# Splitting the last batch's residual, feed-forward and output into two token halves, in an LSH-attention plus FFN kernel

## The chip, the cores and the metric

The kernel runs on one core of a Trainium2 chip. The metric is the device time of one execution in microseconds (us). A core has five engines that each work through their own instruction queue in order: TensorE (PE, matrix products), VectorE (DVE), ScalarE (ACT, activation functions), GpSimd (POOL) and SyncE (SP, which here issues the DMAs). They wait for one another by semaphores.

## The reference, cut to what matters

There are 16 batches of 512 tokens with 128 features. Each batch goes through an attention block and a feed-forward block, both with a layer norm before and after and a residual around:

```python
x = x + ln(attn(ln(x)))          # 16 heads of 8; softmax over scores times a bucket coefficient
x = x + ln(ffn(ln(x)))
# attn: q, v from two 128x128 products; buckets are the signs of q against 6 hyperplanes
#       scores = q q^T / sqrt(128); coeff = 62 + (bucket_s == bucket_t); softmax(scores*coeff) v
# ffn:  h = silu(x W1^T * s1) * (x W2^T * s2)      128 -> 512
#       h = gelu(h H1^T * t1);  h = gelu(h H2^T * t2)   512 -> 512, twice
#       y = h W3^T * s3                            512 -> 128
```

All of it is float32 outside; the scores use a split of q in three bfloat16 parts.

## The kernel before

**Tiling.** A batch is held as `[128, NT, E]` with `NT = 4`: partition p holds tokens 4p to 4p+3, so "tile t" means every fourth token. A norm works tile by tile over 128 features. In the FFN the tokens lie along the free axis: `xnt` is `[128, 512]`, `h` is `[128, NC, 512]` with `NC = 4` blocks ("c") of hidden units. One hidden block of a 512x512 layer is four products (i = 0 to 3) accumulated in one PSUM bank, and a float32 product is two MATMUL instructions in the trace.

**Order of the work.** The program is written by a small planner, the class `Order`. Every piece of the kernel is a Python generator that yields operations (`pe`, `dve`, `act`, `pool`, `dma`), each with an assumed cost, a rank and a function that emits the instructions. The planner advances an assumed clock and lets each engine take the ready operation of lowest rank, first come first served within a rank. ACT takes the one with the lowest time ready plus rank, with 4 us added if it needs another function table. What comes out is one fixed order for each engine; on the chip the engines follow it and wait only for their data. Ranks on PE are 0 for scores, 1 for the weighing with v, 2 for projections and transposes, 4 for the FFN: the FFN fills what attention leaves.

**Buffers are taken in the plan.** `get(pool)` waits in the plan until a named buffer is put back, in order of asking. The pools that matter here: `banks` (2 PSUM banks for transposes, normed values, weighing), `ffn_banks` (3 PSUM banks), `h_bufs` (3), `a_bufs` (2, for the SiLU results), `x1_bufs` (2, the sum after attention, held until the batch's output is added), `xnt_bufs` (1, the transposed input of the FFN).

**From attention to output, for each batch b.** `attend` weighs four heads at a time and ends in `divide` (L1004, L1005), which fills a quarter of the tile `o`. After the fourth, `residual(b)` reloads x (tile `xtr`, L1026), and then:

1. `moments(o)`: statistics of o (DVE, L430 and L434), variance plus eps (ACT, L446, `ve_o`), power -1/2 (POOL, L450, `rs_o`), negated mean times that (DVE, L455, `nm_o`).
2. `rescale` of o into a PSUM bank (ACT, L473, `yb`), and only then `get(x1_bufs)`; the add into `x1` (DVE, L1035).
3. `get(xnt_bufs)`, then `norm_transposed`: moments of x1 (`ve_f`, `rs_f`, `nm_f`), `xn_f` (ACT), four PE transposes (L489, `tp_f`), one copy to `xnt_f` (ACT, L493).
4. `ffn(b)` waits until the previous batch has its first 512x512 layer planned (`stages[b - 1][AHEAD]`). Then come the first-stage products with W1 and W2 (PE, L1088, tile `w`), SiLU in pairs (ACT, L1074), the product of the two (DVE, L1057), two layers of 16 products (PE, L1122, `hp`) with GELU in pairs (ACT, L1135), and the last product (PE, L1156, `yp`, 32 MATMULs of 128x128).
5. The output norm: sums and squares of yp (ACT, L397 and L407), `ve_y`, `rs_y`, `nm_y`, `yn` (L473), the add of x1 (DVE, L1180), after which x1's buffer is put back, and one output DMA (L1186).

The pieces of the attention that fill the engines meanwhile are the logits (DVE, L894), the coefficients (DVE, L865), the subtraction of the maximum (POOL, L947), the exponential (ACT, L952), the scores (PE, L847) and the weighing (PE, L973).

```python
    x1_bufs = Pool("x1_", 2)          # residual(b): taken after rescale, before the add at L1035
    xnt_bufs = Pool("xntf", 1)        # residual(b): taken after that add
    ...
    ffn_banks = Pool("f", 3)          # gate, hp, yp: one bank each
```

Of the kernel before, what the change touches and what calls it, by code (L numbers as in the profile page):

```python
# [190 lines left out]
def tile_lsh_attention_ffn(  # L191
# [193 lines left out]
    def moments(src, name, rank, copy=None):  # L385


        q = name[0]
        rs = p2.tile([P, NT], F32, tag=f"rs{q}", name=f"rs_{name}")
        nm = p2.tile([P, NT], F32, tag=f"nm{q}", name=f"nm_{name}")  # L390
        if copy is not None:

            sums = p2.tile([P, 2, NT], F32, tag=f"su{q}", name=f"su_{name}")

            def sum_(ts_):
                for t in ts_:
                    nc.scalar.activation(  # L397
                        copy[0][:, t, :],
                        src[:, t, :],
                        AF.Identity,  # L400
                        scale=ROOT / E,
                        accum_out=sums[:, 0, t : t + 1],
                    )

            def square(ts_):
                for t in ts_:
                    nc.scalar.activation(  # L407
                        junk,
                        src[:, t, :],
                        AF.Square,  # L410
                        scale=-1.0 * E,
                        bias=sums[:, 0, t : t + 1],
                        accum_out=sums[:, 1, t : t + 1],
                    )

            yield act(1.0, -2, lambda: sum_((0, 1)))
            yield act(1.0, -2, lambda: sum_((2, 3)))
            src = copy[0]
            copy[1]()
            yield act(1.2, -2, lambda: square((0, 1)))  # L420
            od.loose()
            yield act(1.2, -2, lambda: square((2, 3)))
            mean, var = sums[:, 0, :], sums[:, 1, :]
            factor, sign = float(E) ** -3, -1.0 / E
        else:
            st = p2.tile([P, NT, nc.vector.BN_STATS_DIM], F32, tag=f"st{q}", name=f"st_{name}")

            def stats(ts_):
                for t in ts_:
                    nc.vector.bn_stats(st[:, t, :], src[:, t, :])  # L430

            def aggr():
                for t in range(NT):
                    nc.vector.bn_aggr(mv[:, t, :], st[:, t, :])  # L434

            yield dve(0.46, rank, lambda: stats((0, 1)))
            od.loose()
            yield dve(0.46, rank, lambda: stats((2, 3)))
            mv = p2.tile([P, NT, nc.vector.BN_AGGR_DIM], F32, tag=f"mv{q}", name=f"mv_{name}")
            yield dve(0.7, rank, aggr)  # L440
            mean, var, sign, factor = mv[:, :, 0], mv[:, :, 1], -1.0, 1.0
        ve = p2.tile([P, NT], F32, tag=f"ve{q}", name=f"ve_{name}")
        yield act(
            0.22,
            -5,
            lambda: nc.scalar.activation(  # L446
                ve, var, AF.Identity, bias=eps if factor == 1.0 else eps3, scale=factor
            ),
        )
        yield pool(1.0, 0, lambda: nc.gpsimd.tensor_tensor(rs, ve, mhalf[:, 0], op=ALU.pow))  # L450

        def negate():

            for t in range(NT):
                nc.vector.tensor_scalar(  # L455
                    nm[:, t : t + 1],
                    mean[:, t : t + 1],
                    sign,
                    rs[:, t : t + 1],
                    op0=ALU.mult,  # L460
                    op1=ALU.mult,
                )

        yield dve(0.28, rank, negate)
        return nm, rs

    def rescale(src, dst, scales):
# [13 lines left out]
        yield act(0.88, -2, lambda: emit((0, 1)))  # L481
        yield act(0.88, -2, lambda: emit((2, 3)))

    def turned(xn, xnt_tag, name, k, tp):


        def turn():
            for t in range(NT):
                nc.tensor.transpose(tp[:, ts(t, P)], xn[:, t, :], ident)  # L489

        yield pe(0.5, 2, turn)
        xnt = p1.tile([P, S], F32, tag=xnt_tag, name=f"xnt_{name}")
        yield act(0.5, -2, lambda: nc.scalar.copy(xnt, tp))  # L493
        od.put(banks, k)
        return xnt

    def norm_transposed(src, xnt_tag, name, rank):

        xn = p2.tile([P, NT, E], F32, tag=f"xn{name[0]}", name=f"xn_{name}", bufs=1)
        scales = yield from moments(src, name, rank)  # L500
        yield from rescale(src, lambda t: xn[:, t, :], scales)
        k = yield get(banks)
        return (yield from turned(xn, xnt_tag, name, k, bank(k, f"tp_{name}")))
# [78 lines left out]
    def prep(b):  # L582
# [14 lines left out]
        if b:  # L597
            yield wait(known[b])
            xn = p2.tile([P, NT, E], F32, tag="xna", name=f"xn_a{b}", bufs=1)
            yield from rescale(xt, lambda t: xn[:, t, :], (nm_x[:, b], rs_x[:, b]))  # L600
            k = yield get(banks)
            xnt = yield from turned(xn, "xnta", f"a{b}", k, bank(k, f"tp_a{b}"))
        else:
            xnt = yield from norm_transposed(xt, "xnta", f"a{b}", 1)
# [413 lines left out]
    def residual(b):  # L1018
# [10 lines left out]
        scales = yield from moments(o, f"o{b}", 1)  # L1029
        kb = yield get(banks)  # L1030
        ybt = bank(kb, f"yb_{b}").rearrange("p (t e) -> p t e", t=NT)
        yield from rescale(o, lambda t: ybt[:, t, :], scales)
        k1 = yield get(x1_bufs)
        x1 = p1.tile([P, NT, E], F32, tag=k1, name=f"x1_{b}")
        yield dve(0.6, 1, lambda: nc.vector.tensor_tensor(x1, ybt, xt, op=ALU.add))  # L1035
        od.put(banks, kb)
        kx = yield get(xnt_bufs)
        xnt = yield from norm_transposed(x1, kx, f"f{b}", 1)
        od.spawn(ffn(b, x1, k1, xnt, kx))

    def ffn(b, x1, k1, xnt, kx):
# [4 lines left out]
        kh = yield get(h_bufs)  # L1046
        h = p1.tile([P, NC, S], F32, tag=kh, name=f"h_{b}_0")
        there = events(NC)

        def product(w2, c, half, held, h=h, there=there):  # L1050
            yield wait(half)
            kb, g2 = w2
            a, ka = held[c % 2]
            yield dve(
                0.66,
                1,
                lambda: nc.vector.tensor_tensor(h[:, c, :], g2, a, op=ALU.mult),  # L1057
            )
            od.put(ffn_banks, kb)
# [3 lines left out]
        def silus(c0, gates, half, held):  # L1063
            for _ in gates:
                held.append((yield get(a_bufs)))
            tiles = [
                p1.tile([P, S], F32, tag=ka, name=f"a_{b}_{c0 + i}")
# [3 lines left out]
            def emit():  # L1071
                for i, (a, (_, gp)) in enumerate(zip(tiles, gates)):
# [3 lines left out]
            yield act(1.2, 0, emit, "silu")  # L1076
            for kb, _ in gates:
                od.put(ffn_banks, kb)
            held[:] = zip(tiles, list(held))
            od.set(half)  # L1080

        def gate(which, c):
            kb = yield get(ffn_banks)
            gp = bank(kb, f"{which}_{b}_{c}")
            yield pe(
                0.86,
                4,
                lambda: nc.tensor.matmul(  # L1088
                    gp, lhsT=w_sb[which][:, 0, ts(c, P)], rhs=xnt, start=True, stop=True
                ),  # L1090
            )
            return kb, gp

        for c0 in range(0, NC, 2):
            gates = []
            for c in (c0, c0 + 1):
                gates.append((yield from gate("w1", c)))
            half, held = Event(), []
            od.spawn(silus(c0, gates, half, held))
            for c in (c0, c0 + 1):  # L1100
                w2 = yield from gate("w2", c)
                od.spawn(product(w2, c, half, held))
        od.put(xnt_bufs, kx)
        od.set(stages[b][0])

        for layer in (1, 2):
            w = w_sb[f"h{layer}"]
            hin, khin, before = h, kh, there
            kh = yield get(h_bufs)
            h = p1.tile([P, NC, S], F32, tag=kh, name=f"h_{b}_{layer}")  # L1110
            there = events(NC)
            for c0 in range(0, NC, 2):
                got = []
                for c in (c0, c0 + 1):
                    kb = yield get(ffn_banks)
                    hp = bank(kb, f"hp_{b}_{layer}_{c}")
                    for i in range(NC):
                        yield wait(before[i])
                        yield pe(
                            0.86,  # L1120
# [4 lines left out]
                                rhs=hin[:, i, :],  # L1125
# [4 lines left out]
                    got.append((c, kb, hp))  # L1130

                def gelus(got=got, h=h, there=there, sc=w_sb[f"h{layer}s"]):
                    def emit():
                        for c, _, hp in got:
                            nc.scalar.activation(  # L1135
                                h[:, c, :], hp, AF.Gelu, scale=sc[:, c : c + 1]
                            )

                    yield act(1.2, 0, emit, "gelu")
                    for c, kb, _ in got:  # L1140
                        od.put(ffn_banks, kb)
                        od.set(there[c])

                od.spawn(gelus())
            od.put(h_bufs, khin)
            od.set(stages[b][layer])
# [4 lines left out]
        yp = bank(kb, f"yp_{b}")  # L1151
        for t in range(NT):
# [12 lines left out]
        od.put(h_bufs, kh)  # L1165
        od.set(stages[b][3])


        y = p2.tile([P, NT, E], F32, tag="y", name=f"y_{b}", bufs=1)
# [3 lines left out]
            1,  # L1173
            (y, lambda: od.put(ffn_banks, kb)),
        )
        kn = yield get(banks)
        ybt = bank(kn, f"yn_{b}").rearrange("p (t e) -> p t e", t=NT)
        yield from rescale(y, lambda t: ybt[:, t, :], scales)
        z = y
        yield dve(0.6, 1, lambda: nc.vector.tensor_tensor(z, ybt, x1, op=ALU.add))  # L1180
        od.put(banks, kn)
        od.put(x1_bufs, k1)
# [3 lines left out]
            lambda: nc.sync.dma_start(out=out[b].rearrange("(p t) e -> p t e", t=NT), in_=z),  # L1186
# [134 lines left out]
```

## Time and profile before

| what | value |
|---|---|
| three runs | 1370.01, 1375.74, 1375.81 us; median 1375.74 us |
| the profiled execution | 1373.08 us in all; its span, first to last instruction, 1371.3 us |
| granted TensorE clock | 0.991 of full speed over the span |
| busy share of the span | PE 96%, DVE 90%, POOL 89%, ACT 82% |

The profile is of one execution, so sums made from it stand against 1373.08 us (1371.3 us of span and 1.8 us around it), which is 2.7 us under the median of the runs. Times in a timeline are us from the start of the span. A line of a timeline has start, duration, engine, source line, operation, output and inputs, and how many such instructions are merged; in brackets is how long the engine sat idle before it and for whom. `PEld` is the loading of the stationary operand, which the trace lists apart from the MATMUL.

### The profile page before, as it was taken

The page shows a single profiled execution, that of the slowest core. Times are in us where ns is not written, and L with a number is a line of the kernel's source. Part 1 is how long each engine was busy: PE and PEld are TensorE (multiplying, and loading weights), DVE is VectorE, ACT ScalarE, POOL GpSimd, SP SyncE. Part 2 cuts the span into 40 slices and gives each one's busy share as a digit, 9 for nine tenths or more (in the row PEclk, how much of TensorE's full clock was granted, in tenths as well). Part 3 has the DMA queues.
Part 4 walks back from the last instruction along what each step waited for, and adds up shares of the span by engine and source line. Part 5 has one row for each costly group of instructions (what it writes and reads, how often), then busy time and mean ns, then how long its engine had stood idle before and what let it go on. Part 6 is the DMA issues. An engine that isn't in the chain of part 4 may idle for free.

```text
span 1371.3 us, 21177 instructions
## 1 busy us (share of the span) xinstructions
PE 1317.3 (96%) x5922; PEld 550.9 (40%) x5922; DVE 1236.0 (90%) x3989; ACT 1127.8 (82%) x1607; POOL 1217.1 (89%) x319
## 2 busy tenths in 40 slices
PE   9999999999889999999999999999999999999996
PEld 3433334334334434343434434343434434343443
DVE  5999999999889999999999999999999999998210
ACT  2567798999779888988989888988989888988852
POOL 1599999999999999999999999999999999999400
PEclk9999999999899999999999999999999999999998
DMA  5756455445435455445545455454545454453000
GB/s 143 194 148 157 133 150 145 140 140 141 134 106 153 125 130 142 138 138 132 147 116 147 129 134 135 139 139 135 142 124 141 135 134 135 132 122 101 24 8 8
DMA packets 159837, 175.39 MB, mean 128 GB/s; under 512 B 34280, under 2 KB 117480, under 8 KB 159720
## 3 DMA queue, kind: packets, MB, share of 16 engines
q1 hardware_dynamic: 156909, 170.56, 45.4%
q10 hardware_dynamic: 2811, 3.48, 0.8%
q8 instruction: 47, 0.77, 0.2%
q14 instruction: 70, 0.57, 0.1%
HBM read 154.81 MB, written 19.17 MB: 127 GB/s over the span
## 4 chain that ended last, share of the span: by engine, by line
PE 50%; DVE 24%; POOL 9%; issue 8%; DMA 6%; ACT 2%; SPq 1%; POOLq 0%; DVEq 0%; ACTq 0%
PE hp L1122 18%; PE av L973 12%; DVE l L894 11%; PE sp L847 9%; DVE co L865 8%; POOL l L947 8%; PE w L1088 4%; PE yp L1156 3%; DMA mb<-md 3%; DMA bb<-bkd 1%; DMA qd<-q 1%; PE op L994 1%; PE vp L760 1%; POOL rs_x L561 1%; DMA qr<-qd 1%
## 5 line engine op out<-in xcount | busy, mean ns | idle before, releaser
L947 POOL TENSOR_TENSOR l<-l,mb 128x2048 f32<-128x2048 f32 x256 | 1156.1, 4552 | 43.4 <-DVE mxpad L894 24.0
L894 DVE CUSTOM_DVE_ANT_0 l<-co,sp 128x512 f32<-128x512 bf16 x1024 | 665.7, 681 | 13.8 <-PE av L973 6.9
L952 ACT ACTIVATE l<-l 128x2048 f32<-128x2048 f32 x256 | 484.6, 1907 | 40.9 <-POOL l L947 39.4
L1122 PE MATMUL hp<-h,h 128*128 128x512 f32 x1024 | 498.6, 596 | 0.3 <-ACT h L1135 0.3
L865 DVE TENSOR_SCALAR co<-bb,bj 128x516 bf16<-128x516 bf16 x1024 | 455.0, 472 | 3.3 <-DMA bb<-bkd 3.1
L847 PE MATMUL sp<-qr,ql 72*128 72x512 bf16 x1024 | 358.0, 382 | 26.7 <-DVE mxpad L894 22.5
L1122 PEld LDWEIGHTS hp<-h,h 128*128 128x128 f32 x1024 | 190.1, 190 | 185.6 <-issue 151.6
L973 PE MATMUL av<-l,vaug 128*32 128x512 f32 x2048 | 263.6, 603 | 0.0
L847 PEld LDWEIGHTS <-ql 72*128 72x128 bf16 x1024 | 94.1, 97 | 313.9 <-issue 290.7
L1088 PE MATMUL w<-xnt_f,w 128*128 128x512 f32 x256 | 132.0, 601 | 2.5 <-ACT a L1074 2.4
L952 ACT ACT_TABLE_LOAD x86 | 110.3, 1283 | 1.5
L1251 PE MATMUL activity<-still 128*128 128x512 bf16 x402 | 106.6, 385 | 1.0 <-DVE still L280 1.0
L973 PEld LDWEIGHTS av<-l,vaug 128*32 128x32 f32 x2048 | 47.4, 109 | 116.5 <-issue 93.9
L894 DVE DVE_READ_ACCUMULATOR2_ANT mxpad<- 128x1 f32 x1024 | 85.7, 84 | 0.0
L450 POOL TENSOR_TENSOR rs_y<-ve_y,mhalf 128x4 f32<-128x4 f32 x16 | 16.1, 1006 | 67.1 <-issue 34.7
L1057 DVE TENSOR_TENSOR h<-w,a 128x512 f32<-128x512 f32 x64 | 43.7, 682 | 35.2 <-PE w L1088 30.3
L1135 ACT ACT_TABLE_LOAD x58 | 74.4, 1283 | 0.9
L987 ACT COPY avs<-av 128x512 f32<-128x512 f32 x64 | 37.0, 578 | 40.0 <-PE av L973 39.9
L1088 PEld LDWEIGHTS w<-xnt_f,w 128*128 128x128 f32 x256 | 46.9, 191 | 53.1 <-issue 21.8
L1156 PEld LDWEIGHTS yp<-w,h 128*128 128x128 f32 x512 | 65.0, 196 | 7.3 <-issue 4.0
L1156 PE MATMUL yp<-w,h 128*128 128x128 f32 x512 | 66.6, 281 | 0.1
L1251 PEld LDWEIGHTS <-still 128*128 128x128 bf16 x402 | 39.1, 99 | 56.5 <-issue 19.0
(94 smaller groups left out, 941.7 us busy)
## 6 DMA issues: line engine op xcount, KB each, us to landing
mb<-md SPq DMA_DIRECT2D x256, 256.0 KB
bb<-bkd SPq DMA_DIRECT2D x256, 130.5 KB
ql<-qd SPq DMA_DIRECT2D x256, 72.0 KB
qr<-qd SPq DMA_DIRECT2D x255, 72.0 KB
qd<-q SPq DMA_DIRECT2D x96, 128.0 KB
xta<-in_L_attn_x_dram SPq DMA_DIRECT2D x16, 256.0 KB
xtr<-in_L_attn_x_dram SPq DMA_DIRECT2D x16, 256.0 KB
out_dram<-y SPq DMA_DIRECT2D x16, 256.0 KB
```

What stands on the lines that cost most here:

```text
L847: nc.tensor.matmul(sp, lhsT=ql[:, ts(t, P)], rhs=qr, start=True, stop=True)
L865: nc.vector.tensor_scalar(co, bb.rearrange("p (r c) -> p r c", c=BP)[:, :, 0:BC], bjs[b][:, c : c + 1], float(NBKT - 2), op0=ALU.is_equal, ...
L894: nc.vector.tensor_tensor_reduce(out=l, in0=co[:, 0:S], in1=sp, scale=1.0, scalar=-3.0e38, op0=ALU.mult, op1=ALU.max, accum_out=mx[:, t : ...
L947: lambda: nc.gpsimd.tensor_tensor(l, l, mb.unsqueeze(1).to_broadcast([P, NT, S]), op=ALU.subtract),
L952: yield act(1.82, 0, lambda: nc.scalar.activation(l, l, AF.Exp, scale=SCALE), "exp")
L973: nc.tensor.matmul(av[k * Q : (k + 1) * Q, :], lhsT=va[:, t, c : c + Q], rhs=ls[gg * GH + k][0][:, t, :], start=(t == 0), stop=(t == NT - 1),)
L1057: lambda: nc.vector.tensor_tensor(h[:, c, :], g2, a, op=ALU.mult),
L1088: lambda: nc.tensor.matmul(gp, lhsT=w_sb[which][:, 0, ts(c, P)], rhs=xnt, start=True, stop=True),
L1122: lambda i=i: nc.tensor.matmul(hp, lhsT=w[:, i, ts(c, P)], rhs=hin[:, i, :], start=(i == 0), stop=(i == NC - 1),),
L1135: nc.scalar.activation(h[:, c, :], hp, AF.Gelu, scale=sc[:, c : c + 1])
L1156: nc.tensor.matmul(yp[:, ts(t, E)], lhsT=h[:, i, ts(t, P)], rhs=w_sb["w3"][:, i, :], start=(i == 0), stop=(i == NC - 1),)
L1251: nc.tensor.matmul(bk, lhsT=still, rhs=still.unsqueeze(1).to_broadcast([P, NT, P]), start=start, stop=stop,)
```

## The change

The last batch (b = 15) is handled in two halves of its tiles, t = 0, 1 and t = 2, 3, from the moments of o to the output DMA; the planner gets two generators, `added(b, tiles, ...)`, where there was one. The other batches go through the same new code with all four tiles. In detail:

- `moments`, `rescale`, `turned` and `norm_transposed` take a tuple of tiles and touch only those. The planner's cost of the power becomes 0.37 + 0.16 n, 1.01 for four tiles (it was 1.0).
- `residual` takes `x1_bufs` and `xnt_bufs` before it starts the moments of o, for every batch; `added` is what follows.
- In the FFN of a half every product is over 256 columns instead of 512, so a 512x512 layer is twice as many instructions. A half takes one PSUM bank for a pair of hidden blocks (`two_banks`), where a whole batch takes one bank for each. For the W1 pair of a whole batch both banks are now taken before the first of the two products; before, the second was asked for after the first product.
- The halves share x1, xnt, the h tiles and y; the second half puts the shared buffers back.
- The output is written by two DMAs of two tiles each.

```diff
-        scales = yield from moments(o, f"o{b}", 1)
-        kb = yield get(banks)
-        ybt = bank(kb, f"yb_{b}").rearrange("p (t e) -> p t e", t=NT)
-        yield from rescale(o, lambda t: ybt[:, t, :], scales)
         k1 = yield get(x1_bufs)
         x1 = p1.tile([P, NT, E], F32, tag=k1, name=f"x1_{b}")
-        yield dve(0.6, 1, lambda: nc.vector.tensor_tensor(x1, ybt, xt, op=ALU.add))
+        kx = yield get(xnt_bufs)
+        xnt = p1.tile([P, S], F32, tag=kx, name=f"xnt_f{b}")
+
+        parts = (ALL,) if b < B - 1 else HALVES
+        hs = []
+        for tiles in parts:
+            od.spawn(added(b, tiles, o, xt, x1, k1, xnt, kx, hs))
+
+    def added(b, tiles, o, xt, x1, k1, xnt, kx, hs):
+        scales = yield from moments(o, f"o{b}", 1, tiles)
+        kb = yield get(banks)
+        ybt = bank(kb, f"yb_{b}_{tiles[0]}").rearrange("p (t e) -> p t e", t=NT)
+        yield from rescale(o, lambda t: ybt[:, t, :], scales, tiles)
+        span = slice(tiles[0], tiles[-1] + 1)
+        yield dve(
+            0.1 + 0.125 * len(tiles),
+            1,
+            lambda: nc.vector.tensor_tensor(
+                x1[:, span], ybt[:, span], xt[:, span], op=ALU.add
+            ),
+        )
         od.put(banks, kb)
-        kx = yield get(xnt_bufs)
-        xnt = yield from norm_transposed(x1, kx, f"f{b}", 1)
-        od.spawn(ffn(b, x1, k1, xnt, kx))
+        yield from norm_transposed(x1, xnt, f"f{b}", 1, tiles)
+        od.spawn(ffn(b, tiles, x1, k1, xnt, kx, hs))
...
+    def ffn(b, tiles, x1, k1, xnt, kx, hs):
+        whole = tiles == ALL
+        n = len(tiles) * P
+        cols = slice(tiles[0] * P, tiles[0] * P + n)
+        cost = 0.86 * n / S
...
+        def layer_out(layer):
+
+            if whole or tiles[0] == 0:
+                kh = yield get(h_bufs)
+                h = p1.tile([P, NC, S], F32, tag=kh, name=f"h_{b}_{layer}")
+                hs.append((h, kh))
+            else:
+                while len(hs) <= layer:
+                    yield ("rest", 0.5)
+            return hs[layer]
+
+        def two_banks(name):
+
+            k0 = yield get(ffn_banks)
+            b0 = bank(k0, f"{name}_{b}_{tiles[0]}_0")
+            if not whole:
+                return [b0[:, 0:n], b0[:, n : 2 * n]], [k0]
+            k1_ = yield get(ffn_banks)
+            return [b0, bank(k1_, f"{name}_{b}_{tiles[0]}_1")], [k0, k1_]
...
         for c0 in range(0, NC, 2):
-            gates = []
-            for c in (c0, c0 + 1):
-                gates.append((yield from gate("w1", c)))
+            gates, kbs = yield from two_banks(f"w1_{c0}")
+            for i in range(2):
+                yield gate("w1", c0 + i, gates[i])
             half, held = Event(), []
-            od.spawn(silus(c0, gates, half, held))
-            for c in (c0, c0 + 1):
-                w2 = yield from gate("w2", c)
-                od.spawn(product(w2, c, half, held))
-        od.put(xnt_bufs, kx)
-        od.set(stages[b][0])
+            od.spawn(silus(c0, gates, kbs, half, held))
+            for i in range(2):
+                if whole or i == 0:
+                    kb = yield get(ffn_banks)
+                    g2 = bank(kb, f"w2_{b}_{tiles[0]}_{c0 + i}")
+                out_ = g2 if whole else g2[:, i * n : (i + 1) * n]
+                yield gate("w2", c0 + i, out_)
+                od.spawn(product(c0 + i, out_, kb if whole or i else None, half, held))
+        if whole or tiles[0]:
+            od.put(xnt_bufs, kx)
+        if whole:
+            od.set(stages[b][0])
...
                             lambda i=i: nc.tensor.matmul(
                                 hp,
                                 lhsT=w[:, i, ts(c, P)],
-                                rhs=hin[:, i, :],
+                                rhs=hin[:, i, cols],
...
         yield dma(
             256,
             2,
-            lambda: nc.sync.dma_start(out=out[b].rearrange("(p t) e -> p t e", t=NT), in_=z),
+            lambda: nc.sync.dma_start(
+                out=out[b].rearrange("(p t) e -> p t e", t=NT)[:, span], in_=z
+            ),
             held=False,
         )
```

## The prediction, as it was put on record before the changed kernel was run

> **What bounds the kernel now.** I read the page first, then windows by stage, then the timeline around each hand-over the diff touches.
>
> Over two whole batches in mid-run (935 to 1091 us) the window table says that no engine has room:
>
> ```profile
> core 0: us, PE busy (x) PEld busy (x) DVE busy (x) ACT busy (x) POOL busy (x), PEclk, DMA share, GB/s
> 935.00:1091.00 156.00, 152.91 (x696) 64.04 (x695) 154.93 (x499) 138.91 (x173) 151.95 (x39) 1.00 0.50 136
> ```
>
> DVE is busy 99.3%, PE 98.0%, POOL 97.4%: attention sets the pace on DVE and POOL, and the FFN fills PE. The same table in shorter windows shows who is left at the end:
>
> ```profile
> 1275.00:1300.00 25.00, 23.87 (x111) 11.96 (x108) 5.29 (x23) 21.29 (x39) 8.50 (x4) 1.00 0.03 12
> 1340.00:1350.00 10.00, 10.00 (x24) 4.37 (x24) 0.00 (x0) 1.76 (x4) 0.00 (x0) 1.00 0.00 0
> 1360.00:1371.00 11.00, 0.66 (x6) 0.46 (x5) 1.27 (x5) 5.15 (x21) 1.01 (x1) 0.68 0.06 24
> ```
>
> From 1292 us, when the last weighing is done, to 1360.7 us PE runs without a gap: what is left of batch 14's FFN, then all of batch 15's. Then PE is done, and one norm runs alone. The timeline shows it:
>
> ```profile
> 1356.55 4.11 PE L1156 MATMUL yp<-w,h 128*128 128x128 f32 x32
> ...
> 1360.69 0.28 ACT L397 ACTIVATE y<-yp 128x128 f32<-128x128 f32 x1 [3.26 <-PE yp L1156]
> ...
> 1361.71 0.41 ACT L407 ACTIVATE junk<-y,su_y 128x128 bf16<-128x128 f32 x1
> ...
> 1363.83 0.30 ACT L446 ACTIVATE ve_y<-su_y,eps 128x4 f32<-128x4 f32 x1
> 1364.26 1.01 POOL L450 TENSOR_TENSOR rs_y<-ve_y,mhalf 128x4 f32<-128x4 f32 x1 [34.67 <-issue]
> 1365.30 0.58 DVE L455 TENSOR_SCALAR nm_y<-su_y,rs_y 128x1 f32<-128x1 f32 x4 [32.43 <-POOL rs_y L450]
> 1365.55 1.95 ACT L473 ACTIVATE yn<-y,nm_y,rs_y 128x128 f32<-128x128 f32 x4 [1.42 <-DVE nm_y L455]
> 1367.52 0.69 DVE L1180 TENSOR_TENSOR y<-yn,x 128x512 f32<-128x512 f32 x1 [1.65 <-ACT yn L473]
> ```
>
> So the end is: PE work left at 1292, plus 10.6 us of serial norm and output (1360.69 to 1371.3). Only the second can be cut by splitting; of the first, splitting can only add or leave holes.
>
> The third thing to see is in the middle of the run. Batch 13's residual:
>
> ```profile
> 1149.88 0.86 DVE L430 BATCH_NORM_STATS2 st_o<-o 128x6 f32<-128x128 f32 x4
> ...
> 1166.20 0.69 DVE L1180 TENSOR_TENSOR y<-yn,x 128x512 f32<-128x512 f32 x1
> 1167.19 0.68 DVE L1035 TENSOR_TENSOR x<-yb,xtr 128x512 f32<-128x512 f32 x1
> ```
>
> The output add of batch 11 (L1180) ends, and x1 of batch 13 (L1035) follows 1.0 us later. It does so for every batch from 4 to 14, 1.0 or 1.2 us behind: the two `x1_bufs` are always full, and o's norm has been computed by then.
>
> **The change part by part.**
>
> *The last norm.* For a half the serial part is, from the rows above: two sums 0.51, two squares 1.06, `ve_y` 0.43, power 0.71, first `nm_y` 0.25, two `yn` 0.99, add 0.42, output DMA 2.75; 7.1 us instead of 10.6. The power for two columns is worked out from the POOL rows: 1.01 us for 4, 2.93 for 16, 6.76 for 40 columns, so 0.16 a column and 0.37 fixed. The add of 256 columns lies between 0.29 (128 columns, L1005) and 0.68 (512). The DMA takes 3.05 us from the add's end, of which about 0.65 is transfer (30% of the DMA engines in a slice of 2.2 us); half goes. Gain 3.45, between 3.1 (the DMA saves nothing) and 3.6. The first half's norm shares ACT: its own ACT work is about 3 us, and the second half's `yp` is half of 3.8 us behind; up to 2 us can fall in the way, I take 0.6. The last `yp` group took 4.11 us against 3.84 for batch 14's (waiting for the last GELU); the other half covers that: 0.3. Net **-3.1 us** (-1 to -4).
>
> *Twice as many PE instructions.* Batch 15 has 64 hp and 16 w MATMULs of 512 columns; they become 160 of 256, each with its own weight load. The rows in the last 80 us:
>
> ```profile
> L1122 PE MATMUL hp<-h,h 128*128 128x512 f32 x122 | 53.3, 593 | 0.0
> L1122 PEld LDWEIGHTS hp<-h,h 128*128 128x128 f32 x122 | 22.9, 190 | 28.6 <-issue 27.6 <-ACT yb L473 0.2 <-ACT ve_f L446 0.2
> ```
>
> The stream of 42 hp MATMULs at 1294.64 takes 18.0 us to the next kind, 0.43 us each, and the loads start beside the MATMULs. Here a rule speaks against the change: the Trainium skill, "TensorE: Matmul & The Clock Gate", Part 3, "What overlaps and what doesn't", says that a weight load overlaps running matmuls only when it addresses another row group. These use the whole array. By the rule each of 80 added loads costs its 0.19 us, 15.2 us, and the kernel would be slower. By the trace they are hidden: 0.19 + 0.43 would give a spacing of 0.62, and it is 0.43. The nearest short row is yp, 128 columns, 32 MATMULs from 1320.06 to the next kind at 1323.74, 0.115 each, just over 0.43/4. Between the two a 256-column one costs 0.215 to 0.22; added **+0.2 us** (0 to 1.1). The measurement decides.
>
> *ACT and DVE.* SiLU and GELU of 256 columns should cost about 0.41 us instead of 0.68 (0.28 for 128 columns in L397): 12 instructions become 24, 1.6 us more on ACT. DVE has 4 more products, POOL 3 more powers, SP one more output DMA (0.34 us to issue). ACT is 18 to 70% busy in the windows from 1300, DVE at most 27%, POOL and SP nearly idle: nothing, as long as PE has other work queued.
>
> *Banks and tables between 1305 and 1325.* That cover can fail. Before, batch 15's xnt comes at 1313.9, when batch 14 has 4 + 8 MATMULs of its second layer left. The halves have shorter chains (o's and x1's norms halved), so the first xnt half comes about 1305 to 1308, when batch 14 still needs two banks for each pair. Three FFNs then ask for three banks: the first half takes one for W1, the second another, the first a third for W2; each frees only after a SiLU. The SiLU waits for a table load (1.28 us) plus 0.8, the GELU of batch 14 for another. Before, ACT loads three tables after 1294; I count six or seven. PE finds nothing ready for 1.5 to 2 us once or twice. The trace of before has the kind: PE's hole at 1266.6 waits 1.25 us for SiLU (`w L1088 [1.25 <-ACT a L1074]`), that at 1283.0 1.13 us. Two such holes: **+2.5 us** (0 to 5).
>
> *The earlier `get(x1_bufs)`, batches 4 to 14.* o's moments and `yb` now wait for the output add of two batches before. Batch 13's o was ready at 1149.9, the buffer at 1166.9. Where that buffer was free, the chain from the first `st_o` to L1035 took 13 to 15 us (batches 0 to 3: 135.67 to 148.87, 211.68 to 225.72). So x1 and xnt come later by about 13 us, or 9 if the output norm, which then no longer shares POOL and ACT with o's norm, is done 3 to 4 us sooner. Behind it waits only the FFN of that batch. Does it matter? Batch 13's xnt is there at 1183.6, its first w at 1189.1, but its first hp only at 1222.6, right behind batch 12's yp (1221.7): 39 us, stretched by batch 12 using the same PE and banks. Uncovered, the stretch from first w to first hp takes 22 to 26 us (169.9 to 192.0, 246.1 to 270.3, 1260.5 to 1286.0). So some 10 us of slack absorbs the delay in mid-run: **0**, bounds 0 to +15. For batch 14 there is no slack (xnt 1258.3, first hp 1286.0). With xnt about 1268 its hp would start near 1290; batch 13's rest gets PE sooner, and PE's holes of 1263 to 1268 and 1283 to 1288 (2.4 us) partly move. PE loses **+2.5 us** (0 to 6) before the final run. A bank of `banks` is no longer held while waiting for x1; that gains nothing I can point to. Taking both W1 banks first delays one product of 0.86 us a batch, inside the same slack. `xnt_bufs` is back at about 1285, before o of batch 15 (1295.4), and x1's buffer comes at 1296.0: no wait for the last batch.
>
> **Sum**: -3.1 + 0.2 + 2.5 + 0 + 2.5 = +2.1 us. On the profiled execution, 1373.1, that is 1375.2; the median of the runs stands 2.7 us higher, so **1377.5 us** after rounding. With the mid-run part at nothing, the ends of the others add up to -4 and +13: 1372 to 1389.
>
> **The rivals.** 0.5% is 6.9 us, about what a measurement of this kernel can tell from no change.
>
> *Slower: the x1 wait isn't absorbed.* The place is PE between two FFNs in mid-run. It decides if the time from x1 to the output add, 153 to 155 us for batches 4 to 13, does not shrink to about 142, so that with the 13 us chain it exceeds two batches of attention (155.9 us). Each of 11 batches then leaves PE about 1.5 us more without FFN work (PE's present loss is about 1.6 us a batch), the last FFN starts that much later: +16 to the -3.1 + 2.7 of the rest, about 1392. For it: lag and buffer have stayed locked for ten batches, PE is 98% busy. Against: the first two batches took 132 and 130 us from x1 to output.
>
> *Faster: no holes.* The planner keeps PE fed, and batch 13's FFN, undisturbed, closes the old holes: -3.1 - 2.4 - 1 to 2, about 1369.
>
> *The halves are not one behind the other.* Both have rank 4 and queue in turn, so they may finish nearly together. Then their norms share ACT and 2 us of the tail's gain are lost: 1379, still no change.
>
> **How the numbers follow.** No measurable change 0.58 (the sum, 0.50, or the halves in step, 0.08), own range 1371 to 1383; slower by the x1 wait or larger holes 0.32; faster by over 0.5% 0.10. The range 1367 to 1393 reaches up to the slower case.
>
> **What would show it.** Right: a last norm of about 7 us after the last yp; 256-column hp spaced 0.215 us; table loads doubled and one or two PE holes of 1 to 2 us around 1305 to 1325; L1035 of batches 4 to 14 about 14 us behind L1180, with PE still 98% busy. Wrong: PE clearly under 97% in 935 to 1091, a batch period above 78 us, or hp spaced over 0.25 us.

## The result: 2.3% slower, and the profile after

The changed kernel takes 1405.82 us (median of 4 runs, 1403.16 to 1406.87) against 1374.92 us before: ratio 1.0231, 95% interval 1.0213 to 1.0249. The forecast was no change and the range ended at 1393; the loss of 31 us is outside it.

The profiled execution spans 1404.0 us. From its page, for each engine: busy time, share of the span and number of instructions; the kernel before, then the changed one.

```profile
PE 1317.3 (96%) x5922; PEld 550.9 (40%) x5922; DVE 1236.0 (90%) x3989; ACT 1127.8 (82%) x1607; POOL 1217.1 (89%) x319
PE 1336.1 (95%) x6002; PEld 569.3 (41%) x6002; DVE 1239.3 (88%) x3995; ACT 1126.2 (80%) x1622; POOL 1218.7 (87%) x322
```

The busy time of DVE and POOL is that of before within 3.3 us; only the span grew. So work was not added on them, they waited. PE is busy 18.8 us longer; its granted clock fell from 0.991 to 0.981 over the span. The window table shows where, in the same two stretches of mid-run, hundreds of us ahead of the last batch:

```profile
core 0: us, PE busy (x) PEld busy (x) DVE busy (x) ACT busy (x) POOL busy (x), PEclk, DMA share, GB/s
935.00:1091.00 156.00, 148.12 (x673) 62.42 (x672) 146.57 (x476) 129.99 (x167) 146.74 (x38) 0.98 0.46 131
1091.00:1245.00 154.00, 148.94 (x666) 61.45 (x665) 149.31 (x485) 133.19 (x163) 148.16 (x39) 0.99 0.44 124
```

In the first of them PE fell from 152.9 to 148.1 us, DVE from 154.9 to 146.6, POOL from 152.0 to 146.7, all together. That looks like engines that wait for one another, not like one that has become the bound. The last batch's fourth quarter of o (L1037; L1005 in the kernel before) comes at 1317.9 us instead of 1295.1: 22.7 us are lost before the halves have begun, and about 10 us from there to the end (76.1 before, 86.1 now).

The x1 buffer does what the diff says. Batch 13's output add of batch 11, its own first statistics and x1:

```profile
1196.78 0.69 DVE L1270 TENSOR_TENSOR y<-yn,x 128x512 f32<-128x512 f32 x1
1197.78 0.86 DVE L436 BATCH_NORM_STATS2 st_o<-o 128x6 f32<-128x128 f32 x4
1208.78 0.69 DVE L1080 TENSOR_TENSOR x<-yb,xtr 128x512 f32<-128x512 f32 x1
```

The statistics of o now follow the output add (they led it by 16 us), and x1 is 12 us behind it instead of 1.

The halves do what they were meant to do. The end of the timeline (L400 and L467 here are L397 and L450 of the kernel before):

```profile
1370.86 21.32 PE L1201 MATMUL hp<-h,h 128*128 128x256 f32 x98
...
1393.34 2.84 PE L1239 MATMUL yp<-w,h 128*128 128x128 f32 x24
...
1396.22 0.28 ACT L400 ACTIVATE y<-yp 128x128 f32<-128x128 f32 x1 [0.25 <-PE yp L1239]
...
1398.39 0.70 POOL L467 TENSOR_TENSOR rs_y<-ve_y,mhalf 128x2 f32<-128x2 f32 x1 [0.54 <-POOL rs_y L467]
...
1400.71 0.42 DVE L1270 TENSOR_TENSOR y<-yn,x 128x256 f32<-128x256 f32 x1 [0.90 <-ACT yn L493]
```

From the second half's first sum to the end of the span it takes 7.8 us, where the whole batch took 10.6. The first half's sums begin at 1394.43, 1.8 us ahead of the second's at 1396.22, so the two norms share ACT at the end. The 98 products of 256 columns run to 1392.02, 0.216 us each.

### The profile page after: what moved, and what is told of

It is laid out like the page before. It is cut to its first block, busy times and chain, and to the rows that moved or that the text cites. A ratio compares the mean times of both kernels' runs of the same rounds, so it can differ in the third digit from the quotient of the medians.

```text
span 1404.0 us, 21324 instructions
## 1 busy us (share of the span) xinstructions
PE 1336.1 (95%) x6002; PEld 569.3 (41%) x6002; DVE 1239.3 (88%) x3995; ACT 1126.2 (80%) x1622; POOL 1218.7 (87%) x322
## 4 chain that ended last, share of the span: by engine, by line
PE 58%; DVE 22%; DMA 6%; POOL 5%; issue 5%; ACT 3%; SPq 1%; POOLq 0%; DVEq 0%; ACTq 0%
PE hp L1201 24%; PE av L1005 14%; PE sp L879 10%; DVE l L926 10%; DVE co L897 7%; POOL l L979 4%; PE w L1157 4%; DMA mb<-md 4%; PE yp L1239 2%; PE op L1026 1%; DMA bb<-bkd 1%; ACT l L984 1%; DVE h L1127 1%; POOL rs_x L591 1%; DVE mxpad L926 1%
## 5 line engine op out<-in xcount | busy, mean ns | idle before, releaser
L1201 PE MATMUL hp<-h,h 128*128 128x512 f32 (+1 forms) x1088 | 500.4, 573 | 1.0 <-DVE h L1127 0.9
L879 PE MATMUL sp<-qr,ql 72*128 72x512 bf16 x1024 | 362.2, 386 | 49.5 <-DVE mxpad L926 41.4
L1201 PEld LDWEIGHTS hp<-h,h 128*128 128x128 f32 x1088 | 203.5, 191 | 171.3 <-issue 141.2
L1005 PE MATMUL av<-l,vaug 128*32 128x512 f32 x2048 | 270.5, 615 | 0.0
L1157 PE MATMUL w<-xnt_f,w 128*128 128x512 f32 (+1 forms) x272 | 133.5, 587 | 1.3 <-ACT xnt_f L513 0.7
L1005 PEld LDWEIGHTS av<-l,vaug 128*32 128x32 f32 x2048 | 47.0, 110 | 120.8 <-issue 91.4
L467 POOL TENSOR_TENSOR rs_y<-ve_y,mhalf 128x4 f32<-128x4 f32 (+1 forms) x17 | 16.8, 986 | 76.9 <-ACT ve_y L456 76.3
L1157 PEld LDWEIGHTS w<-xnt_f,w 128*128 128x128 f32 x272 | 51.2, 195 | 49.3 <-issue 30.2
L1127 DVE TENSOR_TENSOR h<-w,a 128x512 f32<-128x512 f32 (+1 forms) x68 | 44.3, 655 | 25.6 <-PE w L1157 24.4
```

What stands on the lines that cost most here:

```text
L879: nc.tensor.matmul(sp, lhsT=ql[:, ts(t, P)], rhs=qr, start=True, stop=True)
L1005: nc.tensor.matmul(av[k * Q : (k + 1) * Q, :], lhsT=va[:, t, c : c + Q], rhs=ls[gg * GH + k][0][:, t, :], start=(t == 0), stop=(t == NT - 1),)
L1127: lambda: nc.vector.tensor_tensor(h[:, c, cols], g2, a, op=ALU.mult),
L1157: lambda: nc.tensor.matmul(gp, lhsT=w_sb[which][:, 0, ts(c, P)], rhs=xnt[:, cols], start=True, stop=True),
L1201: lambda i=i: nc.tensor.matmul(hp, lhsT=w[:, i, ts(c, P)], rhs=hin[:, i, cols], start=(i == 0), stop=(i == NC - 1),),
```

## The experiments

Theory A was the prediction's own rival: o's norm waits for x1's buffer, and the middle of the run loses. Theory B: the halves lose it through banks and table loads. Theory C: one of the small edits to all batches does.

**Early buffers alone.** The kernel before with

```diff
+        k1 = yield get(x1_bufs)
+        kx = yield get(xnt_bufs)
         scales = yield from moments(o, f"o{b}", 1)
...
-        k1 = yield get(x1_bufs)
...
-        kx = yield get(xnt_bufs)
```

> The kernel before with one edit: x1's buffer and xnt's buffer are taken before o's moments, for every batch; nothing else of the change. Theory A (o's norm waiting for the output add of two batches before slows the middle of the run): most of the loss is here, 1395 to 1410 us, L1035 about 14 us behind L1180, DVE 95 to 97% busy between 935 and 1091. Theory B (the halves lose it through banks and tables): 1372 to 1379. Theory C (the W1 pair taking both banks, or the planner's order shifted by a cost of 1.01 for 1.0): 1372 to 1379 too.

Measured: 1379.1 us, ratio 1.0047 (1.0032 to 1.0062): 6.5 us, a fifth of the loss. Theory A as the main cause falls. Its windows, and the second window in the kernel before:

```profile
935.00:1091.00 156.00, 153.38 (x698) 64.16 (x697) 154.75 (x507) 139.67 (x175) 153.13 (x39) 1.00 0.48 136
1091.00:1245.00 154.00, 150.16 (x670) 62.04 (x669) 150.04 (x483) 132.79 (x164) 149.73 (x39) 0.99 0.45 128
```

```profile
1091.00:1245.00 154.00, 150.06 (x678) 62.07 (x677) 152.87 (x496) 134.12 (x164) 153.51 (x40) 1.00 0.49 133
```

Up to 1091 us PE, DVE and POOL are as busy as before; after that DVE loses 2.8 us and POOL 3.8. x1 of batch 13 comes at 1174.4 instead of 1167.2. From x1 to the output add it now takes 135 to 147 us (batches 4 to 12) where it took 153 to 155 for most of them: the slack that the prediction counted on is there. But attention is held up late in the run, and the last batch's o is ready 8.5 us later than before (1303.6 instead of 1295.1).

**x1's buffer early, xnt's late.** The same without moving `kx`.

> The kernel before with only x1's buffer taken before o's moments; xnt's buffer stays behind the add. Theory A: as slow as with both, within 5 us, since xnt's buffer is back long before x1's. If xnt's buffer is the wait that counts: 1372 to 1380. Theories B and C: 1372 to 1379.

Measured: 1379.2 us, ratio 1.0045 (1.003 to 1.006). The kept traces show why it is the same: the order of instructions on PE, ACT, DVE and POOL is that of the run before, one by one. So what the early buffers cost comes from x1's; taking xnt's early adds nothing.

**The changed kernel with late buffers.** Batches 0 to 14 take `k1` after `rescale` and `kx` after the add.

```diff
+        if b < B - 1:
+            od.spawn(added(b, ALL, o, xt, None, None, None, None, []))
+            return
         k1 = yield get(x1_bufs)
...
+        if x1 is None:
+            k1 = yield get(x1_bufs)
+            x1 = p1.tile([P, NT, E], F32, tag=k1, name=f"x1_{b}")
```

> The changed kernel, but batches 0 to 14 take x1's buffer after rescale and xnt's after the add, as before the change; the last batch is in halves as changed. Theory A: the loss is gone, 1368 to 1378, with a last norm of 7 to 8 us. Theory B: about as slow as the changed kernel, 1395 to 1410. Theory C: 1390 to 1410 too, with the loss in mid-run.

Measured: 1404.5 us, ratio 1.0234 (1.0219 to 1.0249). Nothing comes back. Beside the larger loss the early buffers cost nothing that shows.

**The changed kernel without halves.** `parts = (ALL,)` for the last batch too.

> The changed kernel with the last batch whole; early buffers, both W1 banks first and the cost of 1.01 stay. Theory A and theory C: 1400 to 1415, a few us above or at the changed kernel, since only the last norm's gain is missing. Theory B: 1372 to 1379.

Measured: 1409.05 us, ratio 1.0262 (1.0244 to 1.0279). Theory B falls: without the halves it is 3 to 4 us slower still. The loss is in code that all batches share.

**Both banks for W1 first.** One edit to the kernel before, in the loop over pairs of W1 products:

```diff
-            gates = []
-            for c in (c0, c0 + 1):
-                gates.append((yield from gate("w1", c)))
+            kbs = []
+            for c in (c0, c0 + 1):
+                kbs.append((yield get(ffn_banks)))
+            gates = []
+            for c, kb in zip((c0, c0 + 1), kbs):
+                gates.append((yield from gate("w1", c, kb)))
```

> The kernel before with one edit: each W1 pair asks for both of its PSUM banks before its first product. Theory C1 (this hold-and-wait on the three FFN banks is the loss): 1392 to 1404 us, DVE near 95% busy between 935 and 1091 and PE throttled to half clock several times in mid-run. Theory C2 (the planner's order tips over on the cost of 1.01, or on the order in which a GELU gives back banks and hands on blocks): 1370 to 1376.

Measured: 1405.4 us, ratio 1.0247 (1.0232 to 1.0262). This edit alone costs as much as the whole change. The time is 1.4 us above theory C1's range and far from C2's; DVE is busy 94.4% between 935 and 1091, and the clock does fall to half several times (see the last section). Batch 6 shows the start of it. The FFN's MATMULs and its activations in the kernel before, from the timeline (scores left out; they too wait for DVE, 0.23, 0.15 and 0.23 us):

```profile
642.71 1.02 PE L1122 MATMUL hp<-h,h 128*128 128x512 f32 x2
643.78 1.02 PE L1088 MATMUL w<-xnt_f,w 128*128 128x512 f32 x2
644.66 1.27 ACT L1135 ACTIVATE h<-hp,h2s 128x512 f32<-128x512 f32 x2
645.65 1.02 PE L1122 MATMUL hp<-h,h 128*128 128x512 f32 x2
647.64 1.02 PE L1088 MATMUL w<-xnt_f,w 128*128 128x512 f32 x2
...
650.47 1.27 ACT L1074 ACTIVATE a<-w,w1s 128x512 f32<-128x512 f32 x2
```

and the same place with both banks first, with some of the scores:

```profile
645.60 1.02 PE L1126 MATMUL hp<-h,h 128*128 128x512 f32 x2
645.97 1.39 ACT L1139 ACTIVATE h<-hp,h2s 128x512 f32<-128x512 f32 x2
647.82 0.38 PE L847 MATMUL sp<-qr,ql 72*128 72x512 bf16 x1 [0.76 <-DVE mxpad L894]
648.43 0.38 PE L847 MATMUL sp<-qr,ql 72*128 72x512 bf16 x1 [0.23 <-DVE mxpad L894]
648.64 1.02 PE L1089 MATMUL w<-xnt_f,w 128*128 128x512 f32 x2
650.03 1.02 PE L1126 MATMUL hp<-h,h 128*128 128x512 f32 x2
651.11 1.02 PE L1089 MATMUL w<-xnt_f,w 128*128 128x512 f32 x2
...
655.23 1.27 ACT L1074 ACTIVATE a<-w,w1s 128x512 f32<-128x512 f32 x2
```

Before, the first W1 product goes with the one free bank, 2.2 us after xnt is there (641.54), while the other two banks wait for batch 5's GELU (644.66). Only the second product is left after the GELU. Now the pair sits on the free bank without using it; PE has only scores between, which wait for DVE (the 0.76 and 0.23 in brackets); and both products come after the GELU, the first 4.0 us after xnt (644.66). From the end of the GELU to the SiLU it was 4.5 us (645.93 to 650.47) and is 7.9 us (647.36 to 655.23). Of these 3.4 us, 2.0 lie ahead of the end of the second product; in the rest ACT does other work first. PE itself idles little more here: 1.1 us from xnt to the SiLU, where it was 0.6. By the code each batch has two such pairs; only this one is read here.

The loss adds up over the batches. Windows of 40 us in mid-run, before:

```profile
920.00:960.00 40.00, 39.14 (x160) 14.79 (x159) 39.58 (x136) 33.53 (x37) 40.00 (x12) 1.00 0.44 125
960.00:1000.00 40.00, 38.73 (x193) 17.82 (x192) 39.93 (x124) 36.49 (x51) 38.63 (x9) 1.00 0.55 142
1000.00:1040.00 40.00, 39.77 (x172) 14.89 (x174) 39.55 (x135) 36.55 (x41) 40.00 (x13) 1.00 0.43 128
```

and with both banks first:

```profile
920.00:960.00 40.00, 38.20 (x170) 16.96 (x168) 38.14 (x125) 28.91 (x40) 37.65 (x10) 0.96 0.45 120
960.00:1000.00 40.00, 38.05 (x166) 14.28 (x158) 36.97 (x121) 31.81 (x38) 37.46 (x11) 0.96 0.53 139
1000.00:1040.00 40.00, 37.33 (x179) 16.45 (x182) 38.75 (x129) 34.43 (x49) 38.72 (x11) 0.96 0.49 128
```

PE is busy 113.6 of 120 us instead of 117.6, and the column PEclk is down to 0.96. The x1 add of a batch, which came 17 to 21 us after the first statistics of its o in the kernel before, comes 20 us after them for batch 6 (609.7 to 629.5), 31 for batch 9 and 59 for batch 14 (1240.2 to 1298.9), going up and down between (30 for batch 11, 62 for batch 12). From x1 to the output add a batch takes 157 to 184 us (batches 4 to 11) instead of 153 to 155. So the FFN falls behind: the last batch's o comes 12 us later than before, and 19 us more are lost from there to the end.

**The early place in line, with the product sent.** The pair asks for its second bank at once, as above, but sends the first product with the first bank.

```diff
+            od.spawn(ask())                               # asks for the second bank now
+            gates = [(yield from gate("w1", c0, k0))]     # and sends the first product
+            yield wait(second)
+            gates.append((yield from gate("w1", c0 + 1, box[0])))
```

> The kernel before; the W1 pair asks for its second bank at once, as with both banks first, but the first product is still sent with the first bank. It keeps the place in the line for banks and gives back the early product. If the bank that lies idle under a product not sent is the loss: 1370 to 1378. If the place in the line is the loss (the pair gets its second bank ahead of the previous batch's products): 1395 to 1408.

Measured: 1372.9 us, ratio 0.9996 (0.9984 to 1.0009). So asking early costs nothing as long as the first product is sent: it is holding the product back until the second bank is there that starts the loss. How it grows to 33 us is not taken apart. The planner's clock moves with the product, and the order it writes changes: with both banks first 1284 of the 2796 DVE instructions compared stand at another place in the order than in the kernel before, from 421 us on, and PE's and ACT's orders change too. With the product sent, DVE and POOL keep the order of before one by one, ACT up to the last batch, and on PE 144 of 5520 MATMULs change places.

**The power's cost of 1.01.**

> The kernel before with the planner's cost of the power at 1.01 instead of 1.0, nothing else. It tells how far the order as such swings on a hundredth of a us. Theory C1: 1369 to 1377. Theory C2 by the cost: 1395 to 1405.

Measured: 1372.7 us, ratio 1.0003 (0.9994 to 1.0012). By itself it does nothing; the order changes in two places.

**Late buffers and single W1 banks, last batch in halves.** The version with late buffers, where whole batches ask for the W1 banks one at a time again.

> The changed kernel with x1's and xnt's buffers taken late and the W1 pair of whole batches asking for its banks one at a time, both as before the change; the last batch stays in halves. Theory C1: the loss is gone, 1366 to 1372, some 3 to 4 us below the kernel before. Theory C2: 1395 to 1405.

Measured: 1370.7 us over 20 runs, ratio 0.9991 (0.9982 to 1.0). The loss is gone, and what is left of the gain is at the edge of what can be told: about 1.2 us by the ratio, where 3 to 4 were expected. It is the best of the versions. Its end, and two windows of its last FFN:

```profile
1358.86 0.28 ACT L400 ACTIVATE y<-yp 128x128 f32<-128x128 f32 x1 [0.25 <-PE yp L1255]
...
1363.35 0.42 DVE L1286 TENSOR_TENSOR y<-yn,x 128x256 f32<-128x256 f32 x1 [0.90 <-ACT yn L493]
```

```profile
1310.00:1320.00 10.00, 9.95 (x32) 5.72 (x32) 1.61 (x4) 5.54 (x9) 0.00 (x0) 1.00 0.00 0
1320.00:1330.00 10.00, 9.50 (x56) 7.78 (x56) 1.70 (x4) 4.76 (x16) 0.00 (x0) 1.00 0.01 2
```

The last norm takes 7.7 us (1358.86 to the span's end, 1366.6), and PE's holes between 1310 and 1330 add up to 0.55 us.

**The changed kernel with single W1 banks.**

> The changed kernel with only the W1 pair of whole batches asking for its banks one at a time. Theory C1: the 6.6 us of the early buffers minus 3 to 4 us of the halves remain, 1373 to 1379. Theory C2: 1395 to 1405.

Measured: 1389.7 us, ratio 1.0126 (1.011 to 1.0143). Neither expectation holds: 16 us come back, but 10 more than the early buffers' cost stay.

**Early buffers and the cost of 1.01.** To see what those 10 us are: the kernel before, early buffers, power at 1.01.

> The kernel before with x1's and xnt's buffers taken early and the power's cost at 1.01. The changed kernel with single W1 banks was at 1389.7, the early buffers alone at 1379.1. If the rest is only the planner's order tipping over once the buffers are taken early: 1384 to 1393. If it belongs to the halves or to the GELU's order of giving back: 1376 to 1382.

Measured: 1394.3 us, ratio 1.015 (1.0126 to 1.0173). The rest comes without halves and without the new order of giving back: the order of instructions is that of the changed kernel with single W1 banks, one by one, up to the last batch. A hundredth of a us in an assumed cost does nothing to the kernel before and 15 us to the one with early buffers, whose order on DVE it changes from 650 us on (971 of 2796 places).

**Two banks for scores and four for the FFN.** The kernel before, and the kernel with both W1 banks first, each with

```diff
-    score_banks = Pool("s", 3)
-    ffn_banks = Pool("f", 3)
+    score_banks = Pool("s", 2)
+    ffn_banks = Pool("f", 4)
```

> The kernel before with two PSUM banks for scores and four for the FFN: the base for the next run. Scores have less lead, so 1375 to 1400 by either theory.

> The same two and four banks, and each W1 pair asks for both banks before its first product. If the loss comes from three banks being too few for a pair that holds one and a pair of the previous batch that needs two: within 5 us of the run with four FFN banks alone. If taking both first costs by itself: 20 us or more above it.

Measured: 1430.5 us, ratio 1.041 (1.0391 to 1.0428), and 1432.0 us, ratio 1.0429 (1.0406 to 1.0452). The traces of the two have the same order on PE, ACT, DVE and POOL, one by one: with a fourth bank, asking for both first changes nothing in the plan. That is the expectation for scarcity. But with two score banks the base is 57 us slower, well above its own expectation, so attention may simply leave the FFN room here. The pair is consistent with scarcity and does not prove it.

Read together, the traces sort the runs by the order that the planner wrote. The three versions that keep the order of before up to the last batch, but for under 3% of PE's places and next to none elsewhere (single W1 banks with late buffers, the cost of 1.01 alone, the product sent early) take the time of before within 0.1%. Every version with another order is slower, by 6 to 58 us, and those that share an order agree within 5 us.

## Why the prediction was wrong, point by point

- *"Taking both W1 banks first delays one product of 0.86 us a batch, inside the same slack."* This is the step that failed. It was seen and priced at nothing; alone it costs 33 us (ratio 1.0247). There are two pairs in a batch, not one product. And the delay isn't inside the slack: with this edit alone the time from x1 to the output add grows to 157 to 184 us from 153 to 155, on a PE with 1.6 us to spare a batch. Two products of 0.86 us in 16 batches would be 27.5 us, near what was measured, but no run shows that the loss is this sum: at batch 6's first pair PE idles only 0.5 us more.
- *The order taken as fixed.* Behind that price stands an assumption that is nowhere said: that each small edit delays one operation in an order that stays. The planner writes the order anew. Both banks first, the early buffers, and the cost of 1.01 on top of them each gave another order from some point on, and each cost time. Taking the W1 edit out of the changed kernel returned only 16 us of the 31.
- *"The earlier get(x1_bufs)": 0 in mid-run, +2.5 at the end.* Alone it measured 6.5 us, above the chosen value, just over the +6 of the end's bound, and it was lost ahead of the last batch's o. The slack argument itself held in early_gets (135 to 147 us from x1 to the output add). What was missed is that it makes the planned order fragile: with the cost of 1.01 the ratio is 1.015. Why that order is so much worse was not settled.
- *The rival "the x1 wait isn't absorbed", 16 us at 0.32.* It had the right side and the right place (PE between two FFNs, a lag that grows), and the wrong edit: with late buffers the changed kernel stayed at 1404.5. Its own test, whether the time from x1 to the output add shrinks to about 142, went against it in early_gets. Its reading "153 to 155 us for batches 4 to 13" holds for batches 4 to 11; batch 12 took 150.6 and batch 13 128.2.
- *The sums.* 1375.2 plus 2.7 is 1377.9, not 1377.5, and the upper ends without the mid-run part add up to +11, not +13. Neither changes the forecast.
- *The last norm.* Expected 7.1 us plus 0.6 for the other half on ACT, 2.85 saved; measured 7.8 in the changed kernel, 2.8 saved. Right. The power for two columns took 0.70 us (0.69 worked out), the add of 256 columns 0.42.
- *Twice the products, +0.2.* 0.216 us each where 0.215 to 0.22 was expected. The Trainium skill's rule ("TensorE: Matmul & The Clock Gate", Part 3, "What overlaps and what doesn't") would have shown as 0.216 + 0.19 us; the trace decides against it here.
- *Banks and tables, +2.5.* Over-priced. In the version with only the halves, PE's holes add up to 0.55 us in 1310 to 1330, with five table loads after 1292; in the changed kernel they add up to 1.2 us from 1318 to 1392. The count of six or seven table loads was right for the changed kernel: it has six after the last o (1318.4 to 1357.3).
- *What would show it wrong* was named: PE in 935 to 1091 under 97% (it is 94.9%). That sign was right and pointed at mid-run.

So the halves were rightly seen as a small gain: 1.2 us by the ratio of the halves-only version (interval 0 to 2.5), and 3 to 4 us as the difference between the changed kernel and the same without halves, whose order is the same up to the last batch. The 31 us came with the rewriting of the code around them.

## What to carry to other kernels

When a diff generalises code that all batches run, price each re-ordered request per use and multiply by all uses before looking at the part that the change is named for; on a pipeline with three engines 97% busy or more, "inside the slack" has to be shown with the filler that takes its place. Send work as soon as its first buffer is there, rather than ask for a set of buffers before using any. And where a greedy planner writes the order, compare the order before and after, not only the operation that moved, and run each small edit alone, since costs don't add (33, 6.5 and -1 to -4 us became 31).

## What the runs showed of the hardware that was not expected

PE's granted clock falls to half for 3.4 or 6.8 us at a time in mid-run, and more often where PE has more holes. Between 420 and 1360 us this happens once in the kernel before (3.4 us, at 671) and six times in the run with both W1 banks first (24 us in all); the three other runs with the order of before have one such dip or none, the changed kernel six. One of these, in the run with both banks first:

```profile
720.00:730.00 10.00, 7.67 (x36) 3.14 (x33) 9.87 (x32) 8.29 (x12) 10.00 (x3) 0.99 0.44 142
730.00:740.00 10.00, 10.00 (x47) 3.65 (x49) 9.70 (x31) 9.94 (x9) 10.00 (x3) 0.84 0.50 129
```

PE had been idle 2.3 of the 4.5 us from 725.0 to 729.5, the longest hole 1.1 us; from 731 to 733 the granted clock is 0.50, and the pair of W1 MATMULs at 729.17 took 1.36 us instead of 1.02. So a hole in PE can cost more than its own length. It doesn't always: the window from 880 to 920 us of this run has 3.1 us of holes and a clock of 1.00. How much of the 33 us is this can be bounded: an estimate from the mean clocks, (1 - 0.985) x 1402.2 against (1 - 0.991) x 1371.3, gives at most about 9 us lost directly. The rest was not taken apart.
